# A cross attention's order on TensorE: output ahead of the scores, probabilities turned behind them, a projection ahead of the values

## The chip, the core and the metric

The kernel runs on one core of one Trainium2 chip. The metric is the device time of one execution in microseconds. A core has TensorE (PE in the profile, with its weight loads as PEld), VectorE (DVE), ScalarE (ACT), GpSimd (POOL) and SyncE (SP, whose queue issues the DMAs here). Matmuls write to PSUM banks; other engines copy from there to SBUF.

## The reference, cut to what matters

The program is a decoder of four layers with three sublayers each: twelve sublayers over 64 sequences of 64 tokens with 256 channels. The change lies in the eleventh, the cross attention of the last layer:

```python
def _L3_xattn_ref(hidden_states, encoder_hidden_states, attention_mask, Wq, bq, Wk, bk, Wv, bv, Wo, qn_w, kn_w):
    H, NH, NKV, HD, GROUPS = 256, 16, 4, 128, 4
    b, s, _ = hidden_states.shape
    se = encoder_hidden_states.shape[1]
    q = (hidden_states @ Wq + bq).reshape(b, s, NH, HD).transpose(0, 2, 1, 3)
    k = (encoder_hidden_states @ Wk + bk).reshape(b, se, NKV, HD).transpose(0, 2, 1, 3)
    v = (encoder_hidden_states @ Wv + bv).reshape(b, se, NKV, HD).transpose(0, 2, 1, 3)
    k = jnp.repeat(k, GROUPS, axis=1)
    v = jnp.repeat(v, GROUPS, axis=1)
    q = _rmsnorm(q, qn_w)
    k = _rmsnorm(k, kn_w)
    scale = 1.0 / np.sqrt(HD).astype(np.float32)
    scores = jnp.einsum('bhsd,bhed->bhse', q, k) * scale
    scores = scores + attention_mask[:, None, :, :]
    probs = jax.nn.softmax(scores.astype(jnp.float32), axis=-1).astype(q.dtype)
    out = jnp.einsum('bhse,bhed->bhsd', probs, v)
    out = out.transpose(0, 2, 1, 3).reshape(b, s, NH * HD)
    return out @ Wo
...
x = _layernorm(x + _L3_xattn_ref(x, ctx_2048, mask_1xSxS2_ff0, ...), axis=-1)
```

The tenth sublayer, a self attention with 16 heads of 128, shares a loop with it; the twelfth, a feed-forward block, follows.

## The kernel before

The 4096 tokens are cut into 8 groups of 512, a group into 4 tiles of 128 tokens (two sequences each). In the two attentions a tile is worked on in two half-steps of eight heads, `hb` 0 and 1. So each attention has 64 items, in the order group, tile, half. `l3_attentions` (L1735) runs both in one software pipeline: its row of 128 items has the 64 of `l3_attn` (`one`) and then the 64 of `l3_xattn` (`two`); step `i` of the loop works on four items at once, each in another stage. `do(stage, name)` calls the function `name` of the item `i - stage`. With n = 64, steps above n have only items of the eleventh sublayer in stages 0 and 1, and from step n + 3 on in all of them. The first item of `two` has hb 0 and enters in step 64, so in the steady part an even step projects for hb 0 and an odd one for hb 1.

What the functions of `two` do for their item:

- `query(i, u)` (L2008), stage 0: four matmuls project 4 heads of queries into a bank of two (tag `p`), VectorE adds the bias, ScalarE squares, VectorE sums, POOL takes the power -1/2. With u = 0 and hb 0 the keys of the tile are projected first, in the same way, and POOL scales them.
- `late(i)` (L2026), stage 0, for hb 0 alone: the values are projected, VectorE adds the bias, and two DMAs on SP's queue swap the two halves of the partitions into `vs`.
- `turn(i, u)` (L2036), stage 1: four transposes of the queries (tile `qT`), copied from PSUM. `key_turned(i)` (L2039), stage 1, for hb 0 alone: the same for the keys (`kT`), copied by ScalarE. Banks for transposes (tag `tr`) are two.
- `scores(i)` (L2044), stage 1: 16 products into one bank, then on VectorE a multiplication by the queries' norms (L2056), the mask (L2057), the maximum (L2059), the subtraction (L2060), on ScalarE the exponential (L2061), on VectorE the sum and its reciprocal (L2062, L2063), on POOL the multiplication by it (L2064).
- `turned(i)` (L2067), stage 2: four transposes of the probabilities (`pt`) and their copy.
- `values(i)` (L2074), stage 2: the products of values and probabilities into two banks (`y`), copied to `yt` by one engine each.
- `output(i)` (L2093), stage 3: eight products into the accumulator; with hb 1 the sum with x, and after the fourth tile of a group the layernorm.
- `outputs_turned` (stage 3) exists in `one` alone; `end(i)` (L2116) turns the rows of the next group (`xt`), once in eight steps, and prepares the twelfth sublayer.

In the profile a float32 product is two PE instructions, so that `scores` shows as x32 and `output` as x16.

The order on PE is that of the calls: `manual_schedule(engines={PE})`. The other engines' queues are put in order by the framework's planner from readiness, not by the order of the calls[...]. `copy` (L251) alternates between ScalarE and VectorE with each call. A step calls it five times (qT, qT, pt, yt, yt), and a group's turned rows twice, so that in the trace pt is copied by VectorE in odd steps and by ScalarE in even ones.

Of the kernel before, what the change touches and what calls it, by code (L numbers as in the profile page):

```python
# [235 lines left out]
class Decoder:  # L236
# [1498 lines left out]
    def l3_attentions(self, ctx, linear):  # L1735

        wk = ctx.enter_context(self.tc.tile_pool(name="l3a", bufs=2, reuse_waits="tile"))
        steps = [(g, t, hb) for g in range(self.n_groups) for t in range(TG) for hb in range(2)]  # L1740
        n = len(steps)
        none = lambda *a: None
        with self.tc.manual_schedule(engines={mybir.EngineType.PE}):
            one, two = self.l3_attn(wk, steps, linear), self.l3_xattn(wk, steps)
            row = [(one, i) for i in range(n)] + [(two, i) for i in range(n)]
            for i in range(2 * n + 3):
                at = lambda j: row[j] if 0 <= j < len(row) else (None, j)

                def do(stage, name, *a):
                    which, j = at(i - stage)  # L1750
                    if which is not None:
                        getattr(which, name, none)(j, *a)

                turning = i == n
                do(0, "start")
                do(2, "value")
                if i == n + 1:
                    two.load_output()
                do(1, "turn", 0)
                if not turning:  # L1760
                    do(0, "query", 0)
                do(1, "turn", 1)
                if not turning:
                    do(0, "query", 1)
                do(3, "outputs_turned")
                do(1, "key_turned")
                do(0, "key", 0)
                do(2, "turned")
                if not turning:
                    do(0, "late")  # L1770
                if i > n + 2:
                    do(3, "output")
                do(1, "scores")
                do(0, "key", 1)
                if i <= n + 2:
                    do(3, "output")
                do(2, "values")
                if turning:

                    two.load_biases()  # L1780
                    do(0, "query", 0)
                    do(0, "query", 1)
                    do(0, "late")
                do(0, "end")
                if i == n - 2:
                    two.rows(0)
                if i == n - 1:
                    two.load()
# [569 lines left out]
```

## Time and profile before

| what | us |
| --- | --- |
| median of 3 runs (4413.67 to 4418.37) | 4415.44 |
| the profiled execution's own time | 4418.43 |
| its span, first to last instruction | 4416.7 |
| eleventh sublayer alone, about 3240 to 4116 | 876 |
| PE busy in that stretch | 813.87 |
| VectorE busy in that stretch | 619.02 |
| ScalarE, POOL busy in that stretch | 252.56, 274.20 |

The time line's lines give the start in us, the length, the engine, the line of the kernel, the operation, out<-in, the shape, and how many were merged; in brackets stands the idle time before and what ended it. Lengths of PE overlap, since a matmul's end is modelled; the difference between two starts is what a piece takes. A line of the list of waits reads: who waited, for whom, total us, how often, the longest. A line of the windows gives the stretch, its length, and busy time and instructions of PE, PEld, DVE, ACT and POOL, then the granted clock of TensorE, the DMA engines' share and GB/s.

### The profile page before, as it was taken

The numbers are of one execution on the slowest core, as the hardware profiler recorded it, in microseconds if no ns is written. First come the engines' busy times: TensorE is split into PE (matmuls) and PEld (weight loads), VectorE is DVE, ScalarE is ACT, GpSimd is POOL, SyncE is SP. The second block draws the span as 40 slices with busy tenths as digits, with TensorE's granted clock in tenths as the row PEclk, the third lists the DMA queues.
The fourth block names the chain that finished last, engine by engine and source line by source line (L and its number), as shares of the span: only waits on it lengthen the run. The fifth ranks groups of instructions, "written<-read, shape, count | busy, mean of one in ns | idle before, by whom it ended". The sixth has DMA issues, their size and how long they took to land. (4 is left out here: it accounts for less than half of the span.)

```text
span 4416.7 us, 73850 instructions
## 1 busy us (share of the span) xinstructions
PE 4088.2 (93%) x28808; PEld 2650.9 (60%) x28808; DVE 3098.4 (70%) x6239; ACT 2019.1 (46%) x3667; POOL 1462.5 (33%) x1501
## 2 busy tenths in 40 slices
PE   8889998999888999769999999999989999999898
PEld 6645566666665555436666666666656666666566
DVE  6744548888674677877777777776767766777576
ACT  5646545667424666544444444444322222232344
POOL 4411121332421111035555555555523333333111
PEclk9989999999999999989999999999999999999899
DMA  2100012333100000111111111111210000000000
GB/s 83 65 20 10 1 41 67 85 69 76 41 2 20 1 1 1 38 34 25 30 25 30 25 30 25 30 25 30 73 48 11 11 10 11 10 11 10 8 15 17
DMA packets 99686, 128.26 MB, mean 29 GB/s; under 512 B 14917, under 2 KB 72453, under 8 KB 97929
## 3 DMA queue, kind: packets, MB, share of 16 engines
q1 hardware_dynamic: 99336, 123.53, 11.2%
q8 instruction: 228, 3.74, 0.4%
q14 instruction: 122, 0.99, 0.1%
HBM read 61.87 MB, written 19.42 MB: 18 GB/s over the span
## 5 line engine op out<-in xcount | busy, mean ns | idle before, releaser
L270 POOL TENSOR_TENSOR rstd<-rstd,neg_half 128x4 f32<-128x4 f32 (+1 forms) x171 | 149.1, 872 | 732.1 <-DVE rstd L268 666.6
L270 POOL TENSOR_TENSOR hrq<-hrq,neg_half 128x4 f32<-128x4 f32 x256 | 258.3, 1009 | 309.0 <-DVE hrq L268 298.0
L1153 DVE TENSOR_REDUCE mc<-sq 128x2 f32<-128x512 f32 x512 | 317.0, 681 | 61.0 <-PE sk L1151 60.7
L1159 ACT ACTIVATE e<-sk 128x512 f32<-128x512 f32 x512 | 265.1, 607 | 110.9 <-PE sk L1151 110.2
L1148 PE MATMUL sq<-l1x 32*128 32x256 f32 x2048 | 274.0, 405 | 4.9 <-DVE z L1034 3.1
L1658 PE MATMUL p<-l3a_wq,xt 128*128 128x512 f32 x512 | 244.2, 600 | 11.0 <-DVE v L257 9.9
L1151 PE MATMUL sk<-l1x 32*128 32x256 f32 x2048 | 251.3, 391 | 0.2 <-DMA l1x<-l1x_m 0.2
L1658 PE MATMUL p<-l3a_wk,xt 128*128 128x512 f32 x512 | 247.1, 605 | 0.0
L270 POOL TENSOR_TENSOR hrk<-hrk,neg_half 128x4 f32<-128x4 f32 x160 | 188.0, 1175 | 177.7 <-DVE hrk L268 171.6
L2101 PE MATMUL acc<-l3x_wo,yt 128*128 128x256 f32 x1024 | 245.9, 396 | 0.7 <-ACT yt L255 0.7
L1658 PE MATMUL p<-l3x_wq,xt 128*128 128x512 f32 x512 | 244.7, 601 | 1.1 <-DVE k L2005 0.8
L1148 PEld LDWEIGHTS sq<-l1x 32*128 32x128 f32 x2048 | 207.8, 194 | 57.7 <-issue 22.4
L1658 PE MATMUL p<-l3a_wv,xt 128*128 128x512 f32 x512 | 234.0, 599 | 0.4 <-ACT y L94 0.4
L1918 PE MATMUL acc<-l3a_wproj,yt 128*128 128x256 f32 x1024 | 231.8, 379 | 0.0
L2101 PEld LDWEIGHTS acc<-l3x_wo,yt 128*128 128x128 f32 x1024 | 202.3, 200 | 42.7 <-issue 14.3
L2064 POOL TENSOR_TENSOR s<-s,smx 128x512 f32<-128x512 f32 x64 | 66.7, 1042 | 481.5 <-DVE smx L2063 241.1
L1918 PEld LDWEIGHTS acc<-l3a_wproj,yt 128*128 128x128 f32 x1024 | 194.3, 190 | 52.5 <-issue 29.2
L255 ACT COPY yt<-y 128x512 f32<-128x512 f32 x64 | 37.5, 586 | 383.7 <-PE y L2082 383.7
L276 PEld LDWEIGHTS qT<-ident,q 128*128 128x128 f32 x1024 | 123.2, 141 | 122.3 <-issue 95.8
L1151 PEld LDWEIGHTS sk<-l1x 32*128 32x128 f32 x2048 | 187.7, 186 | 6.8 <-issue 2.5
L276 PE MATMUL pt<-ident,s 128*128 128x128 f32 x768 | 117.4, 284 | 58.5 <-POOL s L2064 46.2
L276 PE MATMUL qT<-ident,q 128*128 128x128 f32 x1024 | 158.2, 277 | 12.4 <-DVE xt L257 6.9
(396 smaller groups left out, 10265.9 us busy)
## 6 DMA issues: line engine op xcount, KB each, us to landing
vs<-v SPq DMA_DIRECT2D x320, 128.0 KB
x<-in_x SPq DMA_DIRECT2D x8, 512.0 KB
ct<-in_ctxT SPq DMA_DIRECT2D x8, 512.0 KB
cn<-in_ctx SPq DMA_DIRECT2D x8, 512.0 KB
l1x<-in_ctx SPq DMA_DIRECT2D x128, 32.0 KB
l1x_x<-x SPq DMA_DIRECT2D x8, 512.0 KB
l1x<-l1x_x SPq DMA_DIRECT2D x128, 32.0 KB
l1x_r<-r SPq DMA_DIRECT2D x128, 32.0 KB
```

The source lines that it names most:

```text
L255: self.nc.scalar.copy(out, in_)
L270: nc.gpsimd.tensor_tensor(out, out, self.neg_half[:, :n], ALU.pow)
L276: self.nc.tensor.transpose(ps[:, j * P : (j + 1) * P], blk, self.ident)
L1148: nc.tensor.matmul(ps[:, n, :], x_[rows, j, part], c_[rows, j, :], start=True, stop=True)
L1151: nc.tensor.matmul(ps[:, n, :], c_[rows, j, part], x_[rows, j, :], start=True, stop=True)
L1153: nc.vector.tensor_reduce(mc[new % 2][:, ra + k, 2 * j : 2 * j + 2], ps, AX.X, ALU.max, negate=True)
L1159: nc.scalar.activation(es[rb + k], ps, AF.Exp, scale=scale)
L1658: self.nc.tensor.matmul(ps, lhs(c), w(c, cols), start=c == 0, stop=c == 1 and bias is None)
L1918: nc.tensor.matmul(acc[:, :D], yts[h % 2][:, h // 2, :], wp[n // 8][:, (n % 8) * D : (n % 8 + 1) * D], start=n == 0, stop=n == 15,)
L2064: nc.gpsimd.tensor_tensor(s, s, wide(sm), ALU.mult)
L2101: nc.tensor.matmul(acc[:, :D], yts[h % 2][:, h // 2, :], w.o[n // 8][:, (n % 8) * D : (n % 8 + 1) * D], start=n == 0, stop=n == 15,)
```

## The change

In steps up to n nothing changes. Above n the calls stand in another order. Before, a step read: qT, queries, qT, queries, keys turned, probabilities turned, values' projection, output, scores, values. After, it reads: qT, queries, keys turned, qT, (even steps) the second queries, output, scores, probabilities turned, then the second queries (odd steps) or the values' projection (even steps), and values. The output of the steps n + 1 and n + 2, which belongs to the tenth sublayer, moves in front of the scores as well.

```diff
                 do(0, "start")
-                do(2, "value")
-                if i == n + 1:
-                    two.load_output()
-                do(1, "turn", 0)
-                if not turning:
+                if i <= n:
+                    do(2, "value")
+                    do(1, "turn", 0)
+                    if not turning:
+                        do(0, "query", 0)
+                    do(1, "turn", 1)
+                    if not turning:
+                        do(0, "query", 1)
+                    do(3, "outputs_turned")
+                    do(0, "key", 0)
+                    do(2, "turned")
+                    do(1, "scores")
+                    do(0, "key", 1)
+                    do(3, "output")
+                    do(2, "values")
+                    if turning:
+
+                        two.load_biases()
+                        do(0, "query", 0)
+                        do(0, "query", 1)
+                        do(0, "late")
+                else:
+                    do(2, "value")
+                    if i == n + 1:
+                        two.load_output()
+                    do(1, "turn", 0)
                     do(0, "query", 0)
-                do(1, "turn", 1)
-                if not turning:
-                    do(0, "query", 1)
-                do(3, "outputs_turned")
-                do(1, "key_turned")
-                do(0, "key", 0)
-                do(2, "turned")
-                if not turning:
-                    do(0, "late")
-                if i > n + 2:
+                    do(1, "key_turned")
+                    do(1, "turn", 1)
+                    odd = i % 2
+                    if not odd:
+                        do(0, "query", 1)
+                    do(3, "outputs_turned")
                     do(3, "output")
-                do(1, "scores")
-                do(0, "key", 1)
-                if i <= n + 2:
-                    do(3, "output")
-                do(2, "values")
-                if turning:
-
-                    two.load_biases()
-                    do(0, "query", 0)
-                    do(0, "query", 1)
-                    do(0, "late")
+                    do(1, "scores")
+                    do(2, "turned")
+                    do(0, *(("query", 1) if odd else ("late",)))
+                    do(2, "values")
                 do(0, "end")
```

## The prediction

> **What bounds the kernel now.** I read three views in this order: the PE rows of the list of waits, cut to the stretch of the changed loop; the time line of PE over two neighbouring steps; and the table of windows, for the clock. All lie between 3240 us, where the eleventh sublayer runs alone, and 4116 us, where the last one begins.
>
> The list of waits, with PE as the engine that waits:
>
> ```profile
> PE pt L276 <- POOL s L2064: 46.2, 26, 5.3
> PE qT L276 <- DVE xt L257: 6.9, 2, 3.5
> PE qT L276 <- ACT xt L255: 4.7, 7, 0.7
> PE acc L2101 <- ACT yt L255: 0.7, 1, 0.7
> PE p L1658 <- DVE k L2005: 0.5, 1, 0.5
> ```
>
> PE stands still for 59 us of the 876, and 46.2 of them are one wait: the transposes of the probabilities (pt) wait for the last step of the softmax, the multiplication on POOL. Everything else that PE needs is there in time. The stretch is PE's, and a time is made by what PE has to do plus these holes.
>
> The time line of PE shows where the hole lies, and what follows it:
>
> ```profile
> 3574.46 0.66 PE L276 MATMUL pt<-ident,s 128*128 128x128 f32 x4 [3.18 <-POOL s L2064]
> 3574.95 5.31 PE L2101 MATMUL acc<-l3x_wo,yt 128*128 128x256 f32 x16
> 3580.19 1.15 PE L2050 MATMUL s<-kT,qT 128*64 128x64 f32 x32
> 3582.36 0.66 PE L276 MATMUL qT<-ident,q 128*128 128x128 f32 x4
> 3582.86 1.88 PE L1658 MATMUL p<-l3x_wkv,ct 128*128 128x512 f32 x4
> 3584.58 1.88 PE L1658 MATMUL p<-l3x_wq,xt 128*128 128x512 f32 x4
> 3586.29 0.60 PE L276 MATMUL qT<-ident,q 128*128 128x128 f32 x4
> 3586.73 1.88 PE L1658 MATMUL p<-l3x_wq,xt 128*128 128x512 f32 x4
> 3588.45 0.60 PE L276 MATMUL pt<-ident,s 128*128 128x128 f32 x4
> 3588.89 1.88 PE L1658 MATMUL p<-l3x_wkv,ct 128*128 128x512 f32 x4
> 3590.61 3.62 PE L2101 MATMUL acc<-l3x_wo,yt 128*128 128x256 f32 x16
> 3594.15 1.15 PE L2050 MATMUL s<-kT,qT 128*64 128x64 f32 x32
> ```
>
> Differences of starts give what each piece takes on PE: a set of four transposes 0.45, a projection 1.72, output 3.55, scores 1.1, values 1.1 (between scores and the next qT). The last ten lines are an even step (it projects keys and values too), 14.0 us; an odd step is 11.2 us without its hole. The odd steps are those that wait: from the end of scores to pt they have only 1.1 + 0.5 + 1.72 + 0.43 + 1.72 + 0.45 = 5.9 us of work, while the softmax takes about 6.7 (scores ended at 3595.25, POOL ended at 3601.99).
>
> The windows, for the clock after a hole and in the steady stretch behind it:
>
> ```profile
> 3357.70:3363.00 5.30, 5.29 (x20) 4.50 (x20) 1.33 (x3) 0.00 (x0) 2.01 (x2) 0.72 0.01 3
> 3363.00:3375.00 12.00, 12.00 (x85) 7.57 (x84) 9.60 (x18) 4.28 (x7) 4.33 (x5) 1.00 0.00 0
> ```
>
> The column behind POOL is the granted clock. After a hole of 3.18 us it is 0.72 for five microseconds, so that the output above took 5.31 us in place of 3.62. The hole costs twice.
>
> [...]all holes of 3.18 us and more in the pt row were followed by slow work, those of 0.76 were not. [...]in the trace pt is copied by DVE (32) and ACT (31) alone.
>
> **The change part by part.** Only steps above n change, those of the eleventh sublayer and two steps of transition. No instruction is added or removed. The copies keep their order of calls (qT, qT, pt, yt, yt), so their engines stay: pt goes to DVE in odd steps and to ACT in even ones.
>
> 1. Probabilities behind the scores. pt now has the outputs and scores of its step as additional cover, less one projection: in odd steps 1.72 (values' projection) + 1.1 + 0.5 + 1.72 + 0.45 + 0.43 + 3.55 + 1.1 plus 0.45 for the pt of the step before = 11.0 us, in even steps 14. Against 6.7, and against 5.9 + 3.18 = 9.1 in the worst steady case (where DVE has the layernorm too), it is enough. The 46.2 us go. The slow work after them: nine outputs lasted 4.62, 5.30, 5.31, 4.85, 5.31, 5.31, 5.31, 5.30 and 5.50, together 14.2 above 9 x 3.62, and three of the pt sets 0.4 more each: 15.5 us. Together **61.7 us**.
>
> 2. A projection between pt and values. Values needs pt in SBUF, so the copy must end within 1.72 us of the transposes. On ACT (even steps) it is 0.59, and ACT's next work, the exponential, comes 2.8 us after the scores: nothing. On DVE (odd) the score chain starts at the same moment as the transposes: L2056, L2057, L2059, L2060 at about 0.7 each. Its order isn't written out by hand; in the trace it takes independent work between the dependent ones (the yt copy, ready 1.1 after the scores, comes after L2059, at 2.1). pt is ready at 0.5, so I place the copy second or third: it ends at 1.4 to 2.1, and values can begin at 2.2. Below: 0, since the cover can't give time. Above: 0.75 where it comes fourth. I take 0.2 x 32 = 6 us.
>
> 3. Output in front. It needs the yt copies. In odd steps the time from values to output is 0.5 + 1.72 + 0.45 + 0.43 = 3.1 us (5.3 before); DVE's copy began 1.1 after values, and the score chain is 2.2 us older by then: nothing. Without that cover it would be 0.7 a step.
>
> 4. Keys turned ahead of the second queries. Two banks hold transposes, so in odd steps the second qT set now waits for the first qT's copy, on DVE, within 2.17 us. In the trace that copy ended 4.1 us after the scores; counted from there it is now wanted at 3.3 + 0.5 + 2.17 = 5.9. Nothing; once a group, with the layernorm on DVE, it ended at 5.2, plus 0.65 for v: 0 to 0.7, I take 0.2 x 8 = 2 us.
>
> 5. late moves behind pt: its VectorE addition and its two DMAs on SP's queue come about 5 us later in the step. Values needs them two steps (25 us) later. Nothing.
>
> 6. The ends. In the last three steps no projection stands between pt, values and output: about 0.7 each for two pt copies and three yt copies, 3.5 in all, of which 0.7 stood before: +2.8. In the two steps of transition the output of the tenth sublayer follows right behind its transposes: a copy of 0.6 each: +1.
>
> Sum: -61.7 + 6 + 2 + 2.8 + 1 = **-50 us**. The profiled execution took 4418.43 (span 4416.7 and 1.7 around it), so 4368 there; the median of the runs is 3.0 lower, 4415.44, which gives **4365 us**. The parts' bounds (nothing new at all, and the two 3.5 us waits for xt gone as well, against 25 us new) give this case 4347 to 4380.
>
> **Rivals.** *Half is given back.* DVE's order places the pt copy fourth, and the first qT copy late: 0.75 x 32 = 24, and 0.5 x 32 = 16 for the qT bank, in place of 8: -18 us, 4397 (4380 to 4408). For it: DVE is 71% busy here (619 of 876), and yt was indeed placed fourth. Against: yt is ready 0.6 later than pt will be.
>
> *The wait before pt becomes a wait before values, and is dearer.* The calls put the score chain ahead of the copy. If both engines keep that order, DVE's copy ends at 0.1 + 2.76 + 0.69 = 3.6, 1.4 late, and ACT's, behind the exponential, at 4.1, 1.95 late: 32 x 3.35 = 107 us in place of the 6: +51, about 4466. It decides against the change from 0.9 us a step on. [...]Against: in the trace ACT's yt and qT copies (3582.46, 3583.06) stand ahead of the exponential (3584.82), which was asked for earlier.
>
> *The change doesn't do what it says:* the softmax is late again because DVE falls behind as PE speeds up, and the wait only moves to another tile. With 18.8 us of DVE work per pair of steps against 25.2 us this needs a bad order: 4413.
>
> **How the numbers follow.** The main case has 0.60, half given back 0.20, the dear wait 0.13, nothing 0.07. A difference of 0.2%, 8.8 us, is what a measurement can tell from none. Faster: 0.60 + 0.20 + 0.01 = 0.81; same: 0.06; slower: 0.13. The range takes in the first two cases: 4347 to 4404.
>
> **What would show it.** Right: the row of pt waiting for POOL is gone from PE's list, outputs of 5.3 us are gone with it, a pair of steps takes about 25.3 us and a group of eight about 103 in place of 108.5 (3406.97 to 3515.48, between the xt waits). PE waits for pt copies (values) of a few us in total. Wrong: a row of values waiting for DVE or ACT pt above 30 us; qT waiting for DVE qT; or holes of over 3 us elsewhere, with slow outputs behind them.

## The result, and the profile after

The changed kernel takes 4366.72 us (median of 4 runs, 4366.16 to 4372.23) against 4415.44: a ratio of 0.9892, with a 95% interval of 0.9875 to 0.9909, or 49 us less. The forecast was 4365.

The list of waits of the changed kernel, with PE as the engine that waits, from 3240 us to the start of the twelfth sublayer at 4065 (who waited, for whom, total us, how often, the longest):

```profile
PE qT L276 <- ACT xt L255: 7.9, 7, 2.3
PE pt L276 <- POOL s L2074: 5.4, 1, 5.4
PE qT L276 <- DVE qT L257: 4.0, 9, 1.8
PE acc L2111 <- DVE yt L257: 1.2, 1, 1.2
PE acc L2111 <- ACT yt L255: 0.9, 2, 0.7
PE y L2092 <- DVE pt L257: 0.8, 1, 0.8
PE y L2092 <- ACT pt L255: 0.7, 1, 0.7
```

The row that stood for 46.2 us and 26 waits is down to one wait of 5.4, in the step behind the transition (the first steps of the eleventh sublayer alone). In the steady steps pt waits for nothing, and values (y) waits for the copy of pt only twice, in the last steps, 0.7 to 0.8 us each.

The time line of PE over an odd step's end and an even step, the second a neighbour of those shown before:

```profile
3567.32 1.15 PE L2060 MATMUL s<-kT,qT 128*64 128x64 f32 x32
3568.40 0.66 PE L276 MATMUL pt<-ident,s 128*128 128x128 f32 x4
3568.89 1.88 PE L1658 MATMUL p<-l3x_wq,xt 128*128 128x512 f32 x4
...
3571.80 0.66 PE L276 MATMUL qT<-ident,q 128*128 128x128 f32 x4
3572.29 1.88 PE L1658 MATMUL p<-l3x_wkv,ct 128*128 128x512 f32 x4
3574.01 1.88 PE L1658 MATMUL p<-l3x_wq,xt 128*128 128x512 f32 x4
3575.73 0.60 PE L276 MATMUL qT<-ident,q 128*128 128x128 f32 x4
3576.16 1.88 PE L1658 MATMUL p<-l3x_wq,xt 128*128 128x512 f32 x4
3577.88 3.62 PE L2111 MATMUL acc<-l3x_wo,yt 128*128 128x256 f32 x16
```

There is no bracket, that is, no idle time, in any of these lines, and output takes 3.62 us. And VectorE's time line at the same place, where the copy of pt had to find its slot:

```profile
3568.52 0.69 DVE L2066 TENSOR_TENSOR s<-s,hrq 128x512 f32<-128x512 f32 x1 [2.21 <-PE s L2060]
3569.13 0.68 DVE L257 COPY pt<-pt 128x512 f32<-128x512 f32 x1
3569.72 0.68 DVE L2067 TENSOR_TENSOR s<-s,mask 128x512 f32<-128x512 f32 x1
```

The copy comes second, behind the first operation of the score chain, and ends at 3569.81, 0.9 us ahead of values (3570.70).

The windows of the steady part, the first line of the kernel before, the second of the changed one, each from its own table (PE, PEld, DVE, ACT, POOL, then the granted clock):

```profile
3290.00:4070.00 780.00, 734.56 (x5169) 504.31 (x5168) 559.34 (x1111) 230.36 (x382) 252.97 (x244) 0.98 0.05 11
```

```profile
3290.00:4040.00 750.00, 738.40 (x5267) 499.17 (x5266) 567.30 (x1133) 220.65 (x388) 259.58 (x249) 1.00 0.05 11
```

PE is busy for 98.5% (738.40 of 750) in place of 94.2%, at a granted clock of 1.00 in place of 0.98. Over the whole span VectorE is busy for 3095.2 us against 3098.4, POOL for 1465.4 against 1462.5: no work went away, the time came out of PE's holes and of the slow work behind them. One group of eight steps (between the transposes of two groups' rows, 3404.82 and 3507.98) takes 103.2 us in place of 108.5.

Executions differ by some microseconds ahead of these sublayers, so below I also give the length of the two attentions, from the first matmul with l3a_wq to the first with l3f_wfc, in the profiled execution of each kernel: 2197.4 us before and 2144.3 after, 53.1 less. A second run of the changed kernel, beside other variants, gave 4366.35 us, in the first of its two ranges, and 2144.5:

> The changed kernel once more, beside the next ones on one chip. If the one call moved in the run e_mid is worth the same as the whole change: 4363 to 4370 us, within 0.2% of e_mid's 4362.4. If the change is better in truth than e_mid by more than noise: below 4358.

### The profile page after: what moved, and what is told of

Same layout as the page of the kernel before. It is cut to its first block, busy times and chain, and to the rows that moved or that the text cites. A ratio compares the mean times of both kernels' runs of the same rounds, so it can differ in the third digit from the quotient of the medians.

```text
span 4365.0 us, 73891 instructions
## 1 busy us (share of the span) xinstructions
PE 4079.3 (93%) x28808; PEld 2634.9 (60%) x28808; DVE 3095.2 (71%) x6239; ACT 2005.0 (46%) x3667; POOL 1465.4 (34%) x1501
## 5 line engine op out<-in xcount | busy, mean ns | idle before, releaser
L2111 PE MATMUL acc<-l3x_wo,yt 128*128 128x256 f32 x1024 | 232.3, 380 | 2.2 <-DVE yt L257 1.2
L2007 ACT ACTIVATE sq<-q 128x512 f32<-128x512 f32 x128 | 80.4, 628 | 296.4 <-DVE q L2015 251.5
L2111 PEld LDWEIGHTS acc<-l3x_wo,yt 128*128 128x128 f32 x1024 | 191.7, 190 | 40.9 <-issue 14.3
L1912 POOL TENSOR_TENSOR hry<-hry,neg_half 128x8 f32<-128x8 f32 x64 | 106.3, 1661 | 183.7 <-DVE hry L1908 183.7
L1187 PE MATMUL ret<-e,vt 128*32 128x256 f32 x2048 | 140.9, 390 | 19.4 <-DVE mc L1153 18.3
```

Of the source, the lines that this page charges most:

```text
L1187: nc.tensor.matmul(ret[32 * r : 32 * r + 32, :], vt[i % 2][:, lc, 4 * r + j, :], es[r][:, lc, :], start=lc == 0, stop=lc == 1,)
L1912: nc.gpsimd.tensor_tensor(r, r, self.neg_half[:, :8], ALU.pow)
L2007: nc.scalar.activation(sq, x, AF.Square)
L2111: nc.tensor.matmul(acc[:, :D], yts[h % 2][:, h // 2, :], w.o[n // 8][:, (n % 8) * D : (n % 8 + 1) * D], start=n == 0, stop=n == 15,)
```

## The experiments

The question after a forecast that came out is whether its reasons did. Three groups of runs: is it the softmax's time that counts; what does the bare copy cost; and what did the parts of small size do.

**One call moved in the kernel before.** The probabilities are turned between output and scores. Nothing else of the change is made.

```diff
-                do(2, "turned")
+                if i <= n + 2:
+                    do(2, "turned")
                 if not turning:
                     do(0, "late")
                 if i > n + 2:
                     do(3, "output")
+                    do(2, "turned")
                 do(1, "scores")
```

> The order of before, with one call moved in the steady steps: the probabilities are turned between output and scores. Theory (the gain is softmax time covered on PE, wherever the cover comes from): the softmax gets 5.9 + 3.55 = 9.4 us of work in odd steps against 6.7 (9.1 with the layernorm), and the copy of pt is covered by the scores (1.1 us against 0.6 to 0.7). The pt wait of 46 us and the slow work behind it go: 4357 to 4370 us, as the changed kernel. Rival (the projection between pt and values, or the keys' earlier place, is needed for the gain): the copy of pt is late in each step, 4385 to 4415 us.

Measured: 4362.4 us, ratio 0.9875 (0.9861 to 0.9890); the attentions take 2139.0 us. PE's list of waits in this run, the rows that belong to the eleventh sublayer:

```profile
PE qT L276 <- DVE xt L257: 6.7, 2, 3.4
PE pt L276 <- POOL s L2066: 5.7, 8, 1.0
...
PE qT L276 <- ACT xt L255: 4.7, 7, 0.7
...
PE acc L2103 <- DVE yt L257: 2.2, 2, 1.8
...
PE y L2084 <- DVE pt L257: 1.8, 3, 0.8
PE acc L2103 <- ACT yt L255: 0.7, 1, 0.7
```

Theory holds, rival falls: a cover of 9.4 us is enough, except with the layernorm, where once a group 0.7 to 1.0 us is left. Neither the projection behind pt nor the keys' place is needed for the gain; the scores (1.08 us) cover the copy (0.59 to 0.68) in all but three steps (the row of y, 1.8 us). The attentions are even 5.3 us shorter than in the changed kernel.

**One multiplication more on POOL in the kernel before.** It multiplies by ones (a tile that is set once, not shown), so that it only adds time to the softmax.

```diff
             nc.gpsimd.tensor_tensor(s, s, wide(sm), ALU.mult)
+            nc.gpsimd.tensor_tensor(s, s, wide(ones), ALU.mult)
             state[i, "s"] = s
```

> The kernel before, with one more multiplication on POOL (by ones) at the end of each softmax, 1.04 us. Theory (odd steps wait for the softmax on PE): each odd step waits 1.1 us more, 32 x 1.1 = 35, and even steps, whose slack is 0.9, 0.2 each: +35 to +45, 4450 to 4462 us. Rival (POOL is off the path, and the pt wait is the image of something else): 4413 to 4422 us.

Measured: 4472.72 us, ratio 1.0124 (1.0103 to 1.0144), 54 us more; the attentions take 50.8 us more. The time line of PE has, in one group, these sets of pt:

```profile
3451.65 0.65 PE L276 MATMUL pt<-ident,s 128*128 128x128 f32 x4 [1.88 <-POOL s L2068]
...
3464.37 0.66 PE L276 MATMUL pt<-ident,s 128*128 128x128 f32 x4 [0.25 <-POOL s L2068]
...
3481.57 1.11 PE L276 MATMUL pt<-ident,s 128*128 128x128 f32 x4 [4.30 <-POOL s L2068]
```

0.76 has become 1.88 and 3.18 has become 4.30, each 1.12 more, and even steps have begun to wait, by 0.25. POOL is the end of the path, in the direction and about the size expected: the sum, 54, came out above the 35 to 45. PE's listed waits for POOL, up to the start of the twelfth sublayer at 4168, come to 84.2 us in 55 waits, against 46.2 in 26: 38 of the 51 us. Slow work behind the longer holes adds some 5 by the lengths on PE's time line. The even steps, which the expectation took as 0.2 us longer, grew by 0.40 to 0.47 (from 13.96), of which only 0.17 to 0.25 is listed as a wait; the rest is about 6 us in all, and the section on the hardware says why the list is short.

**Two and six multiplications more in the changed kernel.** The same edit, with a loop of 2 or 6.

> The changed kernel, with two more multiplications on POOL (by ones) at the end of each softmax, 2.1 us. Theory: the new order leaves odd steps a slack of 4.7 us (2.4 with the layernorm) and even ones 6 us, so this costs nothing: 4364 to 4374 us; the kernel before lost 54 us to one such multiplication. Rival (the slack isn't there, the softmax stays at the path's edge): 4400 us and more.

> The changed kernel, with six more multiplications on POOL at the end of each softmax, 6.3 us. Theory: more than the slack. Odd steps wait 1.6 us (24 of them) or 3.9 (8, with the layernorm, and slow work of 1.7 behind each), even ones 0.3: 38 + 31 + 14 + 10 = 93, about 4460 us (4430 to 4490). Rival (POOL doesn't reach PE in the new order): 4365 to 4375 us.

With two: 4380.37 us (4373.1 to 4381.44), ratio 0.9905 (0.9889 to 0.9922), which is 6 us above the stated range. The profile says where: the transposes of the rows stand at 3407.31 and 3510.48, a group of 103.17 us against 103.16 without them, so in the steady steps 2.1 us of softmax cost nothing. The attentions are 10.8 us longer in all. Of these 6.1 lie ahead of the first wait for xt, where the wait behind the transition grew from 5.4 to 8.8 us; 3.7 in the one group in which VectorE also prepares the twelfth sublayer's first rows (a wait of qT for VectorE of 2.64 us in place of 1.78, and an output of 5.30 in place of 3.62 behind it); and 1.0 at the end. The slack is there in the steady steps, but these places have none.

With six: 4543.5 us, ratio 1.0278 (1.0255 to 1.0301): 177 us more where 93 were expected. The waits of PE from 3270 to 4040 us:

```profile
PE pt L276 <- POOL s L2078: 79.7, 44, 5.1
PE qT L276 <- DVE qT L257: 18.0, 7, 2.7
PE qT L276 <- ACT xt L255: 10.6, 6, 4.0
```

and POOL's time line:

```profile
3574.07 5.52 POOL L2078 TENSOR_TENSOR s<-s,ones 128x512 f32<-128x512 f32 x5
3579.55 1.01 POOL L270 TENSOR_TENSOR hrk<-hrk,neg_half 128x4 f32<-128x4 f32 x1
3580.52 1.04 POOL L2078 TENSOR_TENSOR s<-s,ones 128x512 f32<-128x512 f32 x1
3581.52 1.49 POOL L2029 TENSOR_TENSOR k<-k,hrk 128x512 f32<-128x512 f32 x1
3582.97 2.42 POOL L270 TENSOR_TENSOR hrq<-hrq,neg_half 128x4 f32<-128x4 f32 x2
```

The direction is the theory's; the size isn't, since the expectation counted the softmax alone. The powers for the queries' and keys' norms (hrq, hrk) stand in the same queue: in these lines hrk begins at 3579.55, behind five multiplications of 5.52 us, and hrq at 3582.97. That the waits of qT for VectorE come from this is my reading of the order. Over the whole stretch, to 4241, the waits for POOL come to 123.8 us, 16.9 of them in one wait behind the transition, those of qT for VectorE to 20.8, and the slow work behind the holes is about 38 us more than in the changed kernel by the lengths on PE's time line. The expectation had 14 for slow work, and nothing for that one wait and for qT.

**The copy without cover.** First in all steps: the order of before, with the probabilities turned right behind the scores and values right behind them. Then in the odd steps alone: the changed kernel, with its second queries back in front of the output.

```diff
-                do(2, "turned")
+                if i <= n + 2:
+                    do(2, "turned")
...
                 do(1, "scores")
+                if i > n + 2:
+                    do(2, "turned")
```

```diff
-                    if not odd:
-                        do(0, "query", 1)
+                    do(0, "query", 1)
...
-                    do(0, *(("query", 1) if odd else ("late",)))
+                    do(0, "late")
```

> The order of before, with the probabilities turned right behind the scores and values right behind them: no projection between. Theory: the pt wait for POOL is gone (-62), and each step shows the copy of pt bare, 0.7 on ScalarE and 0.8 to 1.0 on VectorE, 31 of each: +46 to +54. Net -8 to -16: 4400 to 4410 us. Rival 1 (the copy costs nothing, only pt's place counts): 4360 to 4368 us. Rival 2 (the planner puts the copy behind the score chain): above 4440 us.

> The changed kernel, with the second queries of the odd steps back in front of the output, so that in odd steps nothing lies between the probabilities' transposes and values. Theory: 32 bare copies on VectorE at 0.8 to 1.0 us: +26 to +32 on 4367, 4391 to 4400 us. Rival (the projection's place doesn't matter): 4364 to 4370 us.

Measured for the first: 4422.34 us, ratio 1.0009 (1.0002 to 1.0015), which lies outside all three ranges. PE's list of waits:

```profile
PE y L2085 <- DVE pt L257: 28.9, 32, 2.1
PE y L2085 <- ACT pt L255: 21.0, 31, 0.7
PE qT L276 <- DVE xt L257: 15.2, 7, 5.6
```

The wait for POOL is gone, and the bare copies cost 28.9 + 21.0 = 49.9 us, in the middle of the 46 to 54 expected: 0.9 each on VectorE, 0.68 on ScalarE. The waits for xt, now all on VectorE, are 15.2 us against 11.6 before (6.9 for VectorE and 4.7 for ScalarE). What the expectation lacked is not in the list but in the length of the steps: an even step takes 14.85 us against 13.96 before, where 0.68 is listed, and an odd one 12.06 against 10.96, where 0.87 is. So each of the 63 copies costs 0.2 us more than its listed wait, some 13 us (the section on the hardware has two reasons). The gain of this order is given back whole, by the copy (50 and 13) and by xt (4). Rival 1 falls with its row, and rival 2 as well, since VectorE's copy stands second in its queue here too.

Measured for the second: 4399.11 us, ratio 0.9956 (0.9940 to 0.9973), inside the theory's range, with

```profile
PE y L2091 <- DVE pt L257: 29.6, 32, 3.2
```

as its largest row. The projection's place matters where nothing else covers the copy; one of 1.72 us covers it whole.

**The parts of small size.** The changed kernel with before's order kept in the two steps of transition (the calls of before under `if i in (n + 1, n + 2)`), and the changed kernel with the keys turned behind the second qT:

```diff
-                    do(1, "key_turned")
                     do(1, "turn", 1)
+                    do(1, "key_turned")
```

> The changed kernel, with the order of before kept in the two steps of transition (n + 1 and n + 2). Theory: the 5.4 us wait for the softmax behind the transition, and about 2 us of slow work after it, belong to these two steps' new order: 4358 to 4363 us, 4 to 8 less than the changed kernel, and the steady groups stay at 103.15 us. Rival (POOL's reduction over the partitions for the twelfth sublayer's weights, placed there by the planner, makes the wait under either order): 4364 to 4369 us.

> The changed kernel, with the keys turned behind the second qT set, as before. Theory (two banks for transposes: the second set waits for the copy of the set two before): the 0.27 us waits of qT for VectorE's qT copy, 4.0 us in all, are gone: 4360 to 4365 us, and groups of 102.9 us. Rival (those waits come from VectorE's layernorm alone and move to the keys' transposes): 4364 to 4369 us.

The first took 4363.25 us (4357.92 to 4369.01), ratio 0.9873 (0.9855 to 0.9891): its scatter covers both ranges. The profile is clearer: PE has no row of pt waiting for POOL at all, and the groups stay at 103.16 us, but in the transition these rows are larger than in the changed kernel (2.5 and 3.6 us):

```profile
PE yt L276 <- POOL y L1929: 5.1, 2, 4.8
PE y L1911 <- DMA vs<-v: 4.5, 1, 4.5
```

So the 5.4 us wait belongs to the new order of those two steps, and the rival falls, but that order had saved 3 elsewhere: up to the first wait for xt the run is 4.4 us shorter than the changed kernel. Of this 1.7 is lost again in a slow set and projection behind a later wait for xt (2.24 us, at 3720.46), so that the attentions are only 2.7 us shorter (2141.6).

The second took 4371.39 us, ratio 0.9892 (0.9873 to 0.9911), above both ranges, and its groups 103.22: the theory falls. The waits moved to the keys:

```profile
PE kT L276 <- DVE qT L257: 2.2, 6, 0.4
PE kT L276 <- DVE smx L2073: 1.9, 1, 1.9
```

By the order of the calls it had to be so: whichever set comes second is the one that needs the first qT's bank, at the same distance. Only the second queries between them, as before the change, would make it longer; that was not tried in this order. The attentions take 4 us more than in the changed kernel, most of it not from the keys' place: the waits for xt of 2.28 and 2.25 us, the same in both kernels, have slow projections behind them in this run (2.88 and 3.53 us) and not in the changed kernel.

**A version faster than the changed kernel.** The kernel with the one moved call left seven waits of 0.68 us for xt. Here the rows of the next group are turned in front of values as well:

```diff
+                if i > n + 2:
+                    do(0, "end")
                 do(2, "values")
...
-                do(0, "end")
+                if i <= n + 2:
+                    do(0, "end")
```

> As e_mid, and the transposes of the next group's rows stand in front of values in place of behind it. Theory: seven waits of 0.68 us for ScalarE's xt copy are then covered by values (-4.7), the two waits of 3.4 us for VectorE's xt copy shrink by the 1.1 us of values (-2)[...]: 4352 to 4358 us. Rival (the banks make values or the queries' transposes wait in their place): 4361 to 4366 us.

Measured: 4359.88 us (4357.5 to 4362.29), ratio 0.9863 (0.9848 to 0.9877), on the same chip as the changed kernel's 4366.35 (4363.71 to 4369.09): 6.5 us faster, between the ranges of theory and rival, and the attentions take 2136.6 us. Its list from 3270 to 4040 us:

```profile
PE qT L276 <- DVE xt L257: 7.5, 2, 3.8
PE pt L276 <- POOL s L2069: 5.7, 8, 1.0
```

The ScalarE waits are gone. The two for VectorE's xt copy grew a little in place of shrinking, to 3.8 us, so that part of the theory is wrong. In the kernel before VectorE waits there for POOL (the twelfth sublayer's weights) by 1.53, 0.37 and 1.81 us, until 3624.19, and its xt copy begins at 3629.09, 6.9 us after the first transpose of the rows (3622.23):

```profile
3624.19 0.75 DVE L2151 SCALAR_TENSOR_TENSOR l3f_wproj<-l3f_wproj,tthr,ct 128x512 f32<-128x512 f32 x1 [1.81 <-POOL ct L2150]
...
3629.09 0.68 DVE L257 COPY xt<-xt 128x512 f32<-128x512 f32 x1
```

That the same work holds the copy up in this run, and that 1.1 us of values can't make up for it, is my reading. The gain over the one moved call (4362.4, in another batch) is within what the runs scatter.

## Why the prediction was right, point by point

*Step 1, the softmax covered.* Right. The steady waits of 46.2 us are gone, and so are the outputs of 5.3 us: none above 4.2 is left in the eleventh sublayer. The slow work went with the long holes: the clock of the steady part went from 0.98 to 1.00, and in the kernel with one moved call no output took more than 3.72 us. Of this step only the transition was missed: a wait of 5.4 us, and a projection at 3.53 in place of 1.88 us behind it:

```profile
3256.86 1.12 PE L276 MATMUL pt<-ident,s 128*128 128x128 f32 x4 [5.37 <-POOL s L2074]
3257.77 3.53 PE L1658 MATMUL p<-l3x_wq,xt 128*128 128x512 f32 x4
```

POOL's reduction for the twelfth sublayer's weights begins at 3248.58, and its next instruction, a softmax's multiplication whose input was ready at 3249.7, begins at 3255.78. The kernel before has 7.50 us between the same reduction's start (3252.51) and POOL's next instruction (3260.01), and an earlier reduction in the changed kernel 7.38 (3218.78 to 3226.16). That the reduction holds POOL for those 7 us is my inference; the records give it 0.41 us.

*Step 2, the copy behind the score chain.* The choice of second or third place was right: second. The 6 us taken for it were not needed, since in the steady steps values never waits for pt. The fourth place, the bound above, did not come up; with nothing to lie behind, the copies measured 0.9 and 0.68 as waits.

*Steps 3 and 5, output in front and late behind pt.* Nothing was expected, and the list has no wait of output, or of values for vs, in the steady steps.

*Step 4, the banks.* Taken 2 us, measured 4.0: 0.27 once a group where the layernorm stands on VectorE, and one of 1.8.

*Step 6, the ends.* In the last steps +2.9 of the +2.8 expected (1.2 + 0.9 + 0.8 + 0.7 against 0.7 before). The transition was taken as +1, and cost 7 at the softmax, less 3 at the DMA and at POOL.

*Two readings.* An odd step that waits for nothing takes 10.96 us in the kernel before (five of them do), not the 11.2 taken from a step with a hole; the 11.11 of the changed kernel came near it for another reason (next paragraph). And the 0.72 of the clock belongs to another hole, that at 3357.71, whose output took 4.62 us: it is the mean of 0.50 for a part of the window and 1.00 for the rest:

```profile
3357.70:3360.63 2.93, 2.92 (x9) 2.56 (x10) 1.33 (x3) 0.00 (x0) 1.93 (x2) 0.50 0.02 6
3360.63:3363.00 2.37, 2.37 (x12) 1.94 (x11) 0.00 (x0) 0.00 (x0) 0.09 (x1) 1.00 0.00 0
```

*What the sum lacked.* Two terms that nearly cancel. The two xt waits on VectorE with 3.4 us each, and the two slow projections behind them, turned into two of about 2.3 on ScalarE without slow work, some 7 us gained; I had put this into the range only. That nothing slow stands behind them is in part luck, since the same two waits had slow projections behind them in the run with the keys' old place. And the new order of pieces costs 0.15 us a step where nothing waits, about 9 us: an even step takes 14.11 us in the changed kernel (3571.80 to 3585.91, from qT to qT) and 13.96 with the one moved call (3538.78 to 3552.74), an odd one 11.11 and 10.96. The section on the hardware shows where.

Set against the sum, the attentions' -53.1 us are: -61.7 for the softmax, and some -4 of idle time that the list leaves out; 0 in place of +6 for the copy; +4.0 in place of +2 for the banks; +2.9 at the end; about +4 in place of +1 at the transition; and -7 and +9 that were not in it: about -53. So the forecast of -50 against -49 (-53 without what varies ahead of these sublayers) rests on the right main term, 61.7 us. That the small terms, several of them off by 3 to 9 us, cancel so nearly is luck.

*The rivals.* "Half is given back" needed the copy in fourth place: it came second. The dear wait needed the order of the calls: neither engine kept it. "Only moves" is refuted by the list of waits.

## What to carry to other kernels

On an engine whose order is written by hand, count for each handover the work that lies between the producer's last instruction and the consumer, and compare it with the producer's measured latency at its worst step (here 5.9 us against 6.7, and 9.1 with the layernorm): the place that gives cover for both handovers of a tile, in and out, is what to look for, and one moved call can be worth as much as a whole reordering. Give each PSUM copy something to lie behind, since a bare one costs 0.7 to 0.9 us of listed wait a step here, 0.9 to 1.1 in the step's length, and can eat the whole gain. Keep pieces whose weights have less than full size next to each other (scores and values here), since each way in and out cost 0.15 us in these traces. Price a hole on TensorE with the slow work that can stand behind it: here 11 of the 22 holes of 2.12 to 2.72 us had some, and it cost 1.7 us where an output took 5.31 in place of 3.62.

## What the runs showed of the hardware that was not expected

- Changing between weights of 128 x 128 (full size here) and smaller ones cost time without a listed wait. All pieces have weights of 128 x 128, but for scores (64 columns) and values (64 rows). From a piece's start to the next one's, on PE's time line, as medians over the steps without a wait: a projection takes 1.72 us ahead of a full-size piece and 1.81 ahead of values; output 3.46 ahead of pt and 3.55 ahead of scores; a set of transposes 0.44 ahead of a full-size piece and 0.53 ahead of scores. Behind scores or values a set takes 0.49 in place of 0.44. So it is some 0.09 us on the way to the smaller weights and 0.05 on the way back, 0.15 together:

```profile
3546.59 3.62 PE L2103 MATMUL acc<-l3x_wo,yt 128*128 128x256 f32 x16
3550.04 0.60 PE L276 MATMUL pt<-ident,s 128*128 128x128 f32 x4
3550.57 1.15 PE L2052 MATMUL s<-kT,qT 128*64 128x64 f32 x32
```

  These lines are of the kernel with one moved call. There, as in the kernel before, values follow scores directly, one way in and out in each step. In the changed kernel pt and a projection stand between them, so that each step has two: that is its 0.15 us. The run of the bare copy has two as well, with pt between. That it goes by the weights' size is read from which pieces differ; the cause was not tried.
- PE's listed idle time is a little short: between keys (3600.69) and pt (3602.05) in the kernel before lie 1.36 us, of which the keys' set takes 0.45, so 0.91 us were lost where 0.76 are listed. Over 26 waits that is some 4 us.
- The slow clock came in pieces of one length, and a hole's length alone did not decide on it. In the record of the granted clock of the kernel before and of the changed one, each of the 42 and 32 slow stretches has 0.50 and lasts 3.41 us or a whole number of times that (but for the last, which the end of the record cuts), and in one execution all of them start whole numbers of 3.413 us apart, to 0.01 us: in the kernel before, for example, at 3357.22, 3466.45 and 3575.68, twice 109.23 us, or 32 times 3.413. Two windows of that kernel, in the second of these stretches and behind it:

```profile
3466.60:3469.80 3.20, 3.20 (x9) 2.50 (x8) 0.77 (x2) 0.00 (x0) 1.41 (x2) 0.50 0.00 0
3469.95:3475.60 5.65, 5.65 (x64) 4.29 (x63) 2.65 (x5) 1.17 (x2) 0.00 (x0) 1.00 0.01 3
```

  The same hole without slow work in the changed kernel, and with it in the run with the keys' old place:

```profile
3614.51 0.66 PE L276 MATMUL qT<-ident,q 128*128 128x128 f32 x4 [2.28 <-ACT xt L255]
3615.00 1.88 PE L1658 MATMUL p<-l3x_wq,xt 128*128 128x512 f32 x4
...
3614.88 0.66 PE L276 MATMUL qT<-ident,q 128*128 128x128 f32 x4 [2.28 <-ACT xt L255]
3615.37 2.88 PE L1658 MATMUL p<-l3x_wq,xt 128*128 128x512 f32 x4
```

  In the twelve traces, behind 3262 us and ahead of the last three steps, no hole of 1.5 to 2.01 us had slow work behind it; of those of 2.12 to 2.72 us 11 of 22 had; and of the longer ones all but one, of 3.34 us (3718.73, one moved call), while one of 3.37 in the same execution had. In the kernel before a slow stretch starts at each of the nine holes of 3.18 to 3.46 us between 3300 and 4030 us, from 0.70 us ahead of the hole's end (3742.93, at the hole that ends at 3743.63) to 1.22 behind it (3575.68, at 3574.46). In the changed kernel none starts between 3254.26 and 4066.63; counted on from its own starts in steps of 3.413 us, the next would have come 1.57 us behind the end of its hole of 2.28 and 2.66 behind that of 2.25. So it may go by where a hole ends between those starts; this is read off two traces afterwards, and no run tried it.
